# Four graph-attention layers by gathered neighbour lists: feature tables in rank order for the later layers, and masks gathered into that order

## The chip, the cores and the metric

The kernel runs on one core of a Trainium2 chip. A core has a matrix engine (PE), a vector engine (DVE), a scalar engine (ACT), GpSimd (POOL) and a sync engine (SP), which all run their own instructions in order and wait for each other by semaphores. DMAs are issued from the queues of SP, ACT and POOL and are carried out by 16 DMA engines. The metric is the device time of one execution in microseconds; the figure quoted is the median of several runs.

## The reference

Four layers of graph attention on 3327 nodes with 512 features. The adjacency matrix is symmetric, holds ones on its diagonal and is sparse: a node has between some ten and some forty neighbours. Each layer normalises, projects, scores every pair that is joined, takes a softmax over the neighbours, sums their projected features with these weights and adds the result to its input. The layers have 8, 4, 1 and 8 heads; layers two and three apply an ELU.

```python
h = jnp.maximum(_layernorm(x, axis=-1), 0.0)
...
Wh = (H @ W).reshape(n, N_HEADS, D_K)
sl = jnp.einsum('nhd,hd->nh', Wh, a_l)
sr = jnp.einsum('nhd,hd->nh', Wh, a_r)
e = jax.nn.leaky_relu(sl[:, :, None] + sr.T[None, :, :], negative_slope=NEG_SLOPE)
e = jnp.where(mask[:, None, :], e, -jnp.inf)
alpha = jnp.nan_to_num(jax.nn.softmax(e, axis=2), nan=0.0)
out = jnp.einsum('nhm,mhd->nhd', alpha, Wh).reshape(n, OUT_DIM)
...
x = x + ...
```

## The kernel before

The nodes are padded to 3328, 26 tiles of 128. A first stage (`tile_gat_stack`, lines 560 to 777) reads the adjacency matrix once. POOL multiplies each row by descending node numbers (line 679), DVE takes the largest entries of it, and so every node gets the list of its neighbours' numbers. It also counts the neighbours, and from the counts every node gets a rank: rank 0 has the most. Lists are then put into rank order. `Slots` holds them as columns of indices: column k of tile t has the k-th neighbour of the 128 nodes of ranks 128 t to 128 t + 127, and CAPS[t] is the number of columns of that tile, 36 down to 11. Column 0 is the node itself. There are two copies: `idx` holds node numbers, `twice` holds them doubled, because the first layer's table `tabx` has two half-rows for each node: projected features with scores, and the input x. A list that is shorter than its tile's columns is filled up with row 3328, a padding row with a score that gives no weight.

A table row has 528 numbers, two halves of 256 features and 8 scores each: the scores of the node as a target stand from column 256, those as a neighbour from column 520. `tabx` is filled in node order by the first stage (`features`, line 664). The check for lists that are too long branches to another program, `tile_gat_dense`, which does not run with these inputs.

`tile_gat_lists` then runs the four layers. Its tiles are tiles of ranks, worked from 25 down to 0. A tile's columns are cut into groups of four (`Tile`, line 835). `fetch` gathers a group, one indirect DMA on POOL for each column (line 824); in the later layers the node's own row comes by a plain load from `own_d`, which is in rank order. `scored` computes the weights of a group (DVE, then one exp on ACT, line 880). `group` multiplies rows by weights (DVE, line 903) and adds them up with identity matmuls in one bank (PE, line 908). After the last group the steps of `ends` follow, spread over the next steps: mean, residual, normalisation, transposes, projection, and `rows` (line 976), which writes the next layer's row twice: plainly to `own_d` from SP, and by an indirect DMA from POOL (`scatter`, line 829) to the table of the next layer, `tabs`, which is in node order. Two such tables take turns. The last layer scatters its rows to the output in the same way.

A few tiles with the longest lists are not gathered in the later layers: 1, 9 and 2 of them in layers two, three and four. They go over the whole table, tile by tile, with masks (`Several`, `Wholes`), beside the gathering. The masks come from nine entries `Mask` among the first layer's steps: an entry gathers 128 rows of the adjacency matrix by rank, turns them on PE, and writes them as bytes to DRAM, with the rows in node order as the table has them. `Own` is used only if the first layer had such a tile; it has none.

The order is written out by hand for POOL, PE, DVE and ACT (line 1316); SP's order is left to the compiler. In the loop from line 1366 step s first fetches groups until LOOK = 7 steps ahead, then does what was put at its places "first", "scored" and "last". There are seven buffers `g` for groups. A tile's rows are written five steps after its mean, and its scatter stands in POOL's order there, behind the gathers of step s + 6. A layer's gathers read the whole table, so that the first of them waits for all 26 scatters of the layer before.

The lines that set the order of fetches and scatters:

```python
                while fetched < min(len(steps), s + LOOK):
                    steps[fetched][0].fetch()
                    fetched += 1
                do("first")
                if s + 1 < len(steps):
                    steps[s + 1][0].scored(steps[s + 1][1])
                do("scored")
```

Of the kernel before, what the change touches and what calls it, by code (L numbers as in the profile page):

```python
# [11 lines left out]
U8 = mybir.dt.uint8  # L12
# [483 lines left out]
class Slots:  # L496
# [3 lines left out]

    class Part:
# [13 lines left out]
    def __call__(self, t, k, twice=False):  # L515
        for p in self.parts:
            for t0, t1, n, c in p.blocks:
                if t0 <= t < t1:
                    at = c + (t - t0) * n + k
                    return (p.twice if twice else p.idx)[:, at:at + 1]  # L520
# [3 lines left out]
def tile_gat_stack(ctx: ExitStack, tc: tile.TileContext, x, adj, adjT, ws, avs, out):  # L524
# [35 lines left out]
    with ExitStack() as c1:  # L560
# [49 lines left out]
        def late_constants():  # L610
            pad = once.tile([1, 2 * ROW], F32, name="pad")
            nc.gpsimd.memset(pad, 0.0)
            nc.gpsimd.memset(pad[:, ROW - 8:ROW], FAR)
            nc.sync.dma_start(tabx[NP:NP + 1, :], pad)
# [49 lines left out]
        def features(t, vx, xn, ve):  # L664
# [3 lines left out]
                                 scale=rstd)  # L668
            nc.sync.dma_start(tabx[t * P:(t + 1) * P, :], vx)

        count, pieces, last, normed, loads = None, [], None, None, []
        with tc.manual_schedule(engines={mybir.EngineType.Pool, mybir.EngineType.DVE}):
            for t in range(NT):
# [33 lines left out]
                nc.gpsimd.memset(vx[:, ROW + F:], 0.0)  # L707
# [8 lines left out]
        with tc.manual_schedule(engines={mybir.EngineType.Pool, mybir.EngineType.PE,  # L716
# [7 lines left out]
            nc.vector.tensor_add(rank, rank, part)  # L724
            hi = small.tile([P, NT], F32, name="hi", bufs=1)
# [60 lines left out]
def tile_gat_lists(ctx: ExitStack, tc: tile.TileContext, x, adj, ws, avs, out, ident, half, slots, L, low, spare, tabx, tabs):  # L786
# [25 lines left out]
    own_d = [[dram.tile([P, ROW], F32, name=f"own{i}_{t}") for t in range(NT)] for i in range(2)]  # L812
    tabs_v = [dram_disjoint_views(t[:, :], NT) for t in tabs]
    wide = 3 * P
    masks = [dram.tile([NT, P, wide], U8, name=f"mask{p}") for p in range(ND // 3)]
# [19 lines left out]
    class Tile:  # L835
# [10 lines left out]
        def fetch(self):  # L846
# [6 lines left out]
            for q in range(n):  # L853
                if l > 0 and k0 + q == 0:
                    nc.sync.dma_start(g[:, 0, :], own_d[l % 2][t])
# [9 lines left out]
        def scored(self, i):  # L865
# [4 lines left out]
            if i == 0:  # L870
# [4 lines left out]
                nc.vector.tensor_copy(self.s, g[:, self.own, F // 2:F // 2 + H])  # L875
# [5 lines left out]
            if self.l == 0 and i == 0:  # L881
                nc.scalar.activation(xs[self.t], g[:, n, :F], AF.Copy)
# [93 lines left out]
        def rows(self):  # L976
            if self.W is not None:
                v = scaled(nc, self.pv, self.rstd, work)
                nc.sync.dma_start(own_d[(self.l + 1) % 2][self.t], v)
                waiting.append((tabs_v[(self.l + 1) % 2][self.t], self.t, v))  # L980
# [18 lines left out]
    class Mask:  # L999
# [23 lines left out]
        def keep(self, c0, c1):  # L1023
            def piece():
                u = L.bitcast(U8)[:, c0 * P:c1 * P]
                nc.scalar.activation(u, self.pt[:, :(c1 - c0) * P], AF.Copy)
                p, q = divmod(self.t, 3)
                nc.sync.dma_start(masks[p][c0:c1, :, q * P:(q + 1) * P].rearrange("j p c -> p j c"),
                                  u.rearrange("p (j c) -> p j c", c=P))
            return piece  # L1030

        def finish(self, s):
            for i, c0 in enumerate(range(0, NT, 7)):
                c1 = min(c0 + 7, NT)
                later(s + 1 + i, "first", self.turn(c0, c1))
                later(s + 1 + i, "last", self.keep(c0, c1))

# [7 lines left out]
    class Wholes:  # L1045


        def __init__(self, l, W):
            self.l, self.tiles = l, [Whole(l, t, W) for t in range(ND)]
            self.s = pools["e"].tile([P, ND], F32, name="s", bufs=1)  # L1050
            for t in range(ND):
                nc.sync.dma_start(self.s[:, t:t + 1], own_d[l % 2][t][:, F // 2:F // 2 + 1])
# [13 lines left out]
        def load(self, p, j):  # L1066
# [3 lines left out]
            nc.sync.dma_start(mk, masks[p][j])  # L1070
# [72 lines left out]
    class Own:  # L1143


# [288 lines left out]
```

## Time and profile before

| | |
|---|---|
| median of 3 runs | 2498.1 us (2496.62 to 2504.0) |
| the profiled execution | 2956.34 us |
| its span, first to last instruction | 2954.6 us |
| first stage | 0 to about 262 us |
| the four layers | 262 to 1090, 1096 to 1802, 1806 to 2293, 2297 to 2955 us |
| granted PE clock, mean | 0.88 |
| moved by DMA | 612.95 MB |

The profiled execution is 18% longer than the runs that are timed, so that shares and sequences can be read from it, and durations only with care. A row of the page has the line, the engine, the operation, what is written and read, then busy time, mean duration in ns, and the idle time of that engine just before, with what ended it. "issue" is time in which nothing visible was waited for. The page's split of POOL's work by line, apart from those rows that the prediction shows:

```profile
L824 POOL DMA_INDIRECT g<-tabx,twiceb x342 | 325.1, 951 | 142.2 <-issue 94.6
L824 POOL DMA_INDIRECT g<-tab,idxa x297 | 285.0, 960 | 151.6 <-issue 83.8
...
L679 POOL TENSOR_TENSOR key<-a,keys 128x3328 int32<-128x3328 int32 (+1 forms) x29 | 189.3, 6530 | 2.6 <-DVE cand L688 1.3
```

By layer the gathers of table rows are 467, 406, 243 and 382 (columns of the gathered tiles, less the plainly loaded own rows), in 133, 118, 72 and 111 groups.

### The profile page before, as it was taken

The page shows a single profiled execution, that of the slowest core. Times are in us where ns is not written, and L with a number is a line of the kernel's source. Part 1 is how long each engine was busy: PE and PEld are TensorE (multiplying, and loading weights), DVE is VectorE, ACT ScalarE, POOL GpSimd, SP SyncE. Part 2 cuts the span into 40 slices and gives each one's busy share as a digit, 9 for nine tenths or more (in the row PEclk, how much of TensorE's full clock was granted, in tenths as well). Part 3 has the DMA queues.
Part 4 walks back from the last instruction along what each step waited for, and adds up shares of the span by engine and source line. Part 5 has one row for each costly group of instructions (what it writes and reads, how often), then busy time and mean ns, then how long its engine had stood idle before and what let it go on. Part 6 is the DMA issues. An engine that isn't in the chain of part 4 may idle for free. (4 is left out here: it accounts for less than half of the span.)

```text
span 2954.6 us, 26562 instructions
## 1 busy us (share of the span) xinstructions
PE 2226.0 (75%) x6832; PEld 1218.4 (41%) x6832; DVE 1929.8 (65%) x5004; ACT 895.5 (30%) x2347; POOL 1772.6 (60%) x1777
## 2 busy tenths in 40 slices
PE   4776777777766766888878885768795578887887
PEld 2653344433433333444434442334354344444443
DVE  7997756555545545677756664887888366665666
ACT  5881122221221112333322222333333233332321
POOL 7994566666556636666655644565654565655664
PEclk9998889888888888899988988879898788997899
DMA  6985677777666646777766755777775676666774
GB/s 244 330 300 160 185 235 224 235 221 229 197 203 189 197 125 206 221 209 210 205 199 197 216 163 169 228 227 249 213 253 154 190 208 193 203 195 183 206 199 129
DMA packets 253737, 612.95 MB, mean 207 GB/s; under 512 B 91011, under 2 KB 108419, under 8 KB 249222
## 3 DMA queue, kind: packets, MB, share of 16 engines
q0 software_dynamic: 131120, 455.33, 51.9%
q1 hardware_dynamic: 118710, 149.01, 15.8%
q10 hardware_dynamic: 3744, 6.82, 0.7%
q8 instruction: 55, 0.90, 0.1%
q14 instruction: 108, 0.88, 0.1%
HBM read 544.13 MB, written 66.89 MB: 207 GB/s over the span
## 5 line engine op out<-in xcount | busy, mean ns | idle before, releaser
L908 PE MATMUL bank<-m,ident 128*128 128x512 f32 x2608 | 1313.0, 651 | 319.2 <-DVE m L903 173.2
L903 DVE TENSOR_TENSOR m<-g,pw 128x512 f32<-128x512 f32 x1304 | 811.2, 682 | 523.6 <-ACT pw L880 268.8
L824 POOL DMA_INDIRECT g<-tab,idxb x734 | 703.2, 958 | 386.8 <-issue 201.4
L908 PEld LDWEIGHTS bank<-m,ident 128*128 128x128 f32 x2608 | 522.6, 208 | 970.0 <-issue 642.2
L469 PE MATMUL pv<-w,hT 128*128 128x264 f32 x1664 | 434.3, 417 | 77.8 <-ACT hT L458 37.7
L469 PEld LDWEIGHTS pv<-w,hT 128*128 128x128 f32 x1664 | 337.8, 206 | 182.4 <-issue 48.3
L824 POOL DMA_INDIRECT g<-tabx,twiceb x342 | 325.1, 951 | 142.2 <-issue 94.6
L824 POOL DMA_INDIRECT g<-tab,idxa x297 | 285.0, 960 | 151.6 <-issue 83.8
L880 ACT ACTIVATE pw<-z 128x32 f32<-128x32 f32 (+5 forms) x434 | 83.5, 192 | 885.1 <-DVE z L879 376.0
L1107 PE MATMUL whole<-ve,em 128*128 128x512 f32 x468 | 232.6, 647 | 51.5 <-issue 21.6
L832 POOL DMA_INDIRECT tab<-v,idxb x54 | 54.1, 1003 | 234.2 <-ACT v L476 193.7
L679 POOL TENSOR_TENSOR key<-a,keys 128x3328 int32<-128x3328 int32 (+1 forms) x29 | 189.3, 6530 | 2.6 <-DVE cand L688 1.3
L898 DVE SCALAR_TENSOR_TENSOR bank<-g,pw,bank 128x512 f32<-128x512 f32 x243 | 183.3, 754 | 11.2 <-DVE bank L898 2.6
L451 PE MATMUL pt<-ident,xn 128*128 128x128 f32 x416 | 72.1, 301 | 134.4 <-ACT xn L487 46.5
L1107 PEld LDWEIGHTS whole<-ve,em 128*128 128x128 f32 x468 | 93.9, 207 | 167.2 <-issue 124.8
L688 DVE MAX8 cand<-key 128x8 f32<-128x208 int32 x416 | 143.9, 364 | 0.1
L877 DVE TENSOR_TENSOR z<-g,pw 128x32 f32<-128x32 f32 (+5 forms) x434 | 74.6, 172 | 105.4 <-DMA g<-tab,idxa 61.2
L824 POOL DMA_INDIRECT g<-tabx,twicea x99 | 94.8, 957 | 79.7 <-issue 39.4
L451 PEld LDWEIGHTS pt<-ident,xn 128*128 128x128 f32 x416 | 53.0, 153 | 176.9 <-issue 54.3
L476 ACT ACTIVATE v<-pv,rstd 128x528 f32<-128x528 f32 x78 | 54.2, 695 | 215.4 <-PE bank L908 75.6
L458 ACT ACTIVATE hT<-pt 128x512 f32<-128x512 f32 x104 | 61.1, 587 | 175.0 <-remote 107.5
L1248 ACT ACTIVATE spare<-room,low 128x64 f32<-128x64 f32 x208 | 58.0, 337 | 175.3 <-PE bank L908 86.0
(172 smaller groups left out, 2204.1 us busy)
## 6 DMA issues: line engine op xcount, KB each, us to landing
a<-in_adj SPq DMA_DIRECT2D x25, 1664.0 KB
own<-v SPq DMA_DIRECT2D x78, 264.0 KB
ve<-tab SPq DMA_DIRECT2D x78, 264.0 KB
g<-own SPq DMA_DIRECT2D x66, 264.0 KB
tabx<-vx SPq DMA_DIRECT2D x26, 528.0 KB
g<-tab,idxb POOLq DMA_INDIRECT x734
low<-tab SPq DMA_DIRECT2D x52, 132.0 KB
room<-tab SPq DMA_DIRECT2D x52, 132.0 KB
```

The lines of the kernel that those rows point to most:

```text
L451: nc.tensor.transpose(pt[:, k, :], xn[:, k * P:(k + 1) * P], ident)
L458: nc.scalar.activation(hT, pt, AF.Relu)
L469: nc.tensor.matmul(pv[:, s, :HF + 8], hT[:, k, :], W.w[:, k, s, :], start=(k == 0), stop=(k == KC - 1))
L679: nc.gpsimd.tensor_tensor(key[:, c:c + quarter], a[:, c:c + quarter], keys[:, c:c + quarter], OP.mult)
L688: nc.vector.max(cand[:, g * 8:(g + 1) * 8], key[:, g * SEG:(g + 1) * SEG])
L824: nc.gpsimd.indirect_dma_start(out=out_, out_offset=None, in_=table, in_offset=bass.IndirectOffsetOnAxis(ap=which, axis=0))
L877: nc.vector.tensor_tensor(z, g[:, :n, ROW - 8:ROW - 8 + H], self.s.unsqueeze(1).to_broadcast([P, n, H]), OP.add)
L880: nc.scalar.activation(self.wt[:, k0:k0 + n, :H], z, AF.Exp)
L898: nc.vector.scalar_tensor_tensor(acc, v, w, acc, OP.mult, OP.add)
L903: nc.vector.tensor_tensor(m[:, q, :].rearrange("p (s h d) -> p s h d", s=2, d=D), v.rearrange("p s (h d) -> p s h d", d=D), wt[:, k0 + q, ...
L908: nc.tensor.matmul(self.po, ident, m[:, q, :], start=(k0 + q == 0), stop=(k0 + q == K - 1))
L1107: nc.tensor.matmul(tl.po.rearrange("p (s m) -> p s m", s=2), e[:, q * P:(q + 1) * P], v.rearrange("p (s m) -> p s m", s=2)[:, :, :F // 2], ...
```

## The change

The tables of layers two to four are in rank order. A tile's new rows are then 128 neighbouring rows, and one plain DMA from SP writes them to the table; `own_d`, the scatter of rows and the views for it go. The tile's own row and the target scores are loaded from the same place.

The later layers' lists must then hold ranks and not nodes. The first stage writes each node's rank as a number into column 256 of its row in `tabx`, in place of its first target score (one DMA of 26 x 128 single numbers). The 16 columns behind x, which were set to zero by POOL, take a copy of the scores, made by ACT. In the first layer every gathered row so brings the rank of the neighbour along, and after a group's exp ACT copies these numbers, converted to integers, over the group's columns of `idx`. The first layer gathers by `twice` and by column 0, which stay.

The masks' rows must be in rank order too. `Mask` writes its bytes to `found`, with rows in node order. 26 new entries, `Ranked`, gather 128 rows of it (1152 bytes each) by column 0 on POOL into one of three slices of `spare`, and SP writes them to `masks`. Eight of them stand between the last eight groups of the first layer, 18 behind the last group. `Mask` entries stand 10 steps apart and not 11. `Own` goes.

```diff
@@ Slots
-    def __call__(self, t, k, twice=False):
+    def __call__(self, t, k, twice=False, count=1):
...
-                    return (p.twice if twice else p.idx)[:, at:at + 1]
+                    return (p.twice if twice else p.idx)[:, at:at + count]
@@ first stage
+            nc.gpsimd.memset(pad[:, F // 2:F // 2 + 1], float(NP))
...
+            nc.scalar.activation(vx[:, ROW + F:].rearrange("p (s n) -> p s n", s=2), pv[:, :, ROW // 2 - 8:ROW // 2],
+                                 AF.Copy, scale=rstd)
...
-                nc.gpsimd.memset(vx[:, ROW + F:], 0.0)
...
+            nc.sync.dma_start(tabx[:NP, :].rearrange("(t p) c -> p t c", p=P)[:, :, F // 2:F // 2 + 1],
+                              rank.unsqueeze(2))
@@ tile_gat_lists
-    own_d = [[dram.tile([P, ROW], F32, name=f"own{i}_{t}") for t in range(NT)] for i in range(2)]
-    tabs_v = [dram_disjoint_views(t[:, :], NT) for t in tabs]
-    masks = [dram.tile([NT, P, wide], U8, name=f"mask{p}") for p in range(ND // 3)]
+    found = dram.tile([NP, ND * P // 4], I32, name="found")
+    masks = dram.tile([ND // 3, NT, P, wide // 4], I32, name="masks")
@@ Tile.fetch
-                    nc.sync.dma_start(g[:, 0, :], own_d[l % 2][t])
+                    nc.sync.dma_start(g[:, 0, :], tabs[l % 2][t * P:(t + 1) * P, :])
@@ Tile.scored
-                nc.vector.tensor_copy(self.s, g[:, self.own, F // 2:F // 2 + H])
+                nc.vector.tensor_copy(self.s, g[:, n, F:F + H] if self.l == 0 else g[:, 0, F // 2:F // 2 + H])
...
-            if self.l == 0 and i == 0:
-                nc.scalar.activation(xs[self.t], g[:, n, :F], AF.Copy)
+            if self.l == 0:
+                ranks = n - (i == 0)
+                nc.scalar.activation(slots(t, max(k0, 1), count=ranks), g[:, :ranks, F // 2], AF.Copy)
+                if i == 0:
+                    nc.scalar.activation(xs[self.t], g[:, n, :F], AF.Copy)
@@ Tile.rows
-                nc.sync.dma_start(own_d[(self.l + 1) % 2][self.t], v)
-                waiting.append((tabs_v[(self.l + 1) % 2][self.t], self.t, v))
+                nc.sync.dma_start(tabs[(self.l + 1) % 2][self.t * P:(self.t + 1) * P, :], v)
@@ Mask.keep
-                nc.sync.dma_start(masks[p][c0:c1, :, q * P:(q + 1) * P].rearrange("j p c -> p j c"),
-                                  u.rearrange("p (j c) -> p j c", c=P))
+                nc.sync.dma_start(found.rearrange("(j p) c -> p j c", p=P)[:, c0:c1, self.t * n:(self.t + 1) * n],
+                                  u.bitcast(I32).rearrange("p (j c) -> p j c", c=n))
@@ new
+    class Ranked:
...
+        def __init__(self, j):
+            self.j, self.k0 = j, [0]
+
+        def fetch(self):
+            n = ND * P // 4
+            rows = spare[:, self.j % 3 * n:(self.j % 3 + 1) * n].bitcast(I32)
+            gather(rows, found, slots(self.j, 0))
+            nc.sync.dma_start(masks[:, self.j, :, :].rearrange("s p c -> p s c"),
+                              rows.rearrange("p (s c) -> p s c", c=wide // 4))
@@ the loop over layers
-                    steps.insert(18 + 11 * t, (Mask(t), 0))
-            if l == 0 and DENSE[l]:
-                steps.insert(10, (Own(wholes.tiles[0], wholes.s[:, 0, :]), 0))
+                    steps.insert(18 + 10 * t, (Mask(t), 0))
+                steps[-8:] = [s for i, step in enumerate(steps[-8:]) for s in (step, (Ranked(i), 0))]
+                steps += [(Ranked(j), 0) for j in range(8, NT)]
```

The loads of `Wholes` and `Several` take tables and masks from the new places, in the same sizes.

## Prediction

> **What bounds the kernel now.** I read the page first for the engines' totals, then the busy time in the four layer stretches, then the waits, then the timeline at the places that the change touches.
>
> ```profile
> PE 2226.0 (75%) x6832; PEld 1218.4 (41%) x6832; DVE 1929.8 (65%) x5004; ACT 895.5 (30%) x2347; POOL 1772.6 (60%) x1777
> ...
> L824 POOL DMA_INDIRECT g<-tab,idxb x734 | 703.2, 958 | 386.8 <-issue 201.4
> ...
> L832 POOL DMA_INDIRECT tab<-v,idxb x54 | 54.1, 1003 | 234.2 <-ACT v L476 193.7
> ```
>
> No engine is full on the page. POOL's 60% hides something: its indirect DMAs last 0.95 us, but the timeline shows them 1.25 us apart whenever nothing else stops them (0.30 us of "issue" after each), so 77% on this page would already be a full POOL.
>
> ```profile
> 1049.95 0.94 POOL L824 DMA_INDIRECT g<-tabx,twiceb  x1 [0.31 <-issue]
> 1051.20 0.95 POOL L824 DMA_INDIRECT g<-tabx,twiceb  x1 [0.30 <-issue]
> 1067.42 0.99 POOL L832 DMA_INDIRECT tab<-v,idxb  x1 [15.28 <-ACT pw L880]
> 1089.65 0.99 POOL L832 DMA_INDIRECT tab<-v,idxb  x1 [21.24 <-ACT v L476]
> 1096.61 0.99 POOL L824 DMA_INDIRECT g<-tab,idxa  x1 [5.98 <-DMA tab<-v,idxb]
> ```
>
> This is the seam between the first and the second layer: the last gather, two scatters that wait for their rows, then the next layer's first gather, 45 us later. The seam is the compute tail, not POOL's own work.
>
> ```profile
> 262.00:1090.00 828.00, 620.57 (x1740) 310.42 (x1738) 472.37 (x1260) 162.43 (x337) 478.30 (x502) 0.87 0.68 203
> 1096.00:1802.00 706.00, 561.99 (x1604) 298.52 (x1604) 446.78 (x1202) 202.16 (x613) 411.42 (x432) 0.89 0.67 196
> 1806.00:2293.00 487.00, 359.59 (x1027) 201.93 (x1026) 383.84 (x730) 170.32 (x414) 277.86 (x294) 0.86 0.72 224
> 2297.00:2955.00 658.00, 515.75 (x1660) 272.58 (x1660) 398.89 (x837) 182.06 (x633) 391.55 (x408) 0.87 0.66 191
> ```
>
> The columns are length, then PE, weight loads, DVE, ACT and POOL (busy us and count). At 1.25 us each POOL's instructions fill 628, 540, about 355 and 510 us of the four layers, PE's busy time 621, 562, 360 and 516: they are level in all four, and DVE (384) leads in the third.
>
> ```profile
> POOL tab L832 <- ACT v L476: 250.0, 50, 21.2
> POOL g L824 <- DVE m L903: 86.0, 51, 7.9
> ...
> DVE z L877 <- DMA g<-tab,idxa: 61.2, 7, 19.9
> ```
>
> POOL stands 250 us before scatters and 86 us and more before gathers whose buffer the compute still holds. DVE waits for gathered rows 61 us only, in seven places, nearly all at starts of layers. So in this execution gathers arrive in time, and a scatter that blocks POOL costs little: at its place in the order groups up to six steps ahead have been fetched (LOOK = 7, seven buffers), some 30 us of work.
>
> **The profiled time and the median.** The profiled execution took 2956.34 us (span 2954.6), the median is 2498.1: 458 us less. If all of that lies in the four stretches (2679 us), they last 2221 us unprofiled. POOL's 1.25 us x 1615 indirect DMAs are 2019 us, 91% of that, where they are 75% of the profiled stretches. PE's 2058 busy us are 93% at the profiled clock of 0.87. Assuming that neither pace shrinks, POOL is much nearer to being the limit in the run that counts than on the page, with PE beside it. This is an estimate and the weakest step here.
>
> **What the Trainium skill says.** "DMA: Bandwidth & Descriptors", section Issuing engine by pattern, gives indirect transfers to GpSimd and simple stores to Sync; the trace agrees, with 0.99 us of POOL for a scatter and 0.32 us of SP for the plain write of the same rows (own<-v). Its section Issuing engines are not separate DMA queues says that another issuing engine saves only the time to initiate a DMA; so bytes moved from POOL to SP don't by themselves relieve the 16 DMA engines, and the page counts both queues, 51.9% and 15.8%, against the same 16 engines. Its section Rules for kernel authors says a strided last dimension becomes one descriptor per element; the trace holds no such transfer of the rank column's length.
>
> **The change part by part.** Removed: 78 scatters, 26 each for the tables of layers two, three and four. The last layer's 26 scatters to the output stay. The plain own write becomes the table write, so SP's count there is unchanged and 78 x 264 KB (20.6 of 613 MB) are not written twice.
>
> (1) First layer: 26 scatters at 0.99 + 0.30 = 1.29 us free POOL of 34 us; eight of the new mask gathers stand between its last groups, 8 x 1.25 = 10 us. Net 24 us of POOL; with PE level beside it I take three quarters, -18 us (0 to -24).
>
> (2) Second layer: 34 us of POOL, 540 to 506, but PE at 562 doesn't move: I take 0.4, -14 us (0 to -34). Third: DVE is ahead, -5 us (0 to -15). Fourth: no scatter leaves it, 0.
>
> (3) The waits for v that go: worth 0 in themselves. What is late next is the free g buffer, at almost the same place.
>
> (4) Seams two and three: the scatter at 1801.95 is followed by its first dependent gather at 1805.66, 3.7 us; the plain write at 1801.70 let a load of the same rows start at 1803.73, 2.0 us. Two seams, -3 us.
>
> (5) Masks. The nine Mask steps now write node-ordered rows, the same 128-byte pieces. New: 26 gathers of 1152-byte rows by node, each followed by an SP write into rank order, through three slices of one buffer. No row shows this. A turn is a gather's landing (at most 3.95 us: the third gather of the second layer's first group starts at 1099.18, its reader on DVE at 1103.13), a plain write (2.0 us, from (4)) and some 0.3 us of hand-over: 6.2 us for three slices, 2.1 us each. Eighteen stand behind the last group: 38 us. Their cover is the seam, 45 us on the page, or about 30 if compute follows POOL closely (3.95 landing, some 5 for the group, 15 from the last product on DVE at 1074 to the row at 1089, 7 from scatter to gather). The last tile's table write stands on SP behind about twelve of these writes, and the next layer's first own row behind the last. Queued behind a waiting gather on POOL is all of the second layer. Bounds -5 (cover whole, landing 2 us earlier) and +60 (5 us each); I take +10.
>
> (6) List turning: 133 ACT copies of 128x4 or less, at the 0.19 us of the small ACT rows, 26 us on an engine with 162 busy of 828. Each stands behind the exp that DVE waits for, one step ahead of its use, so it is hidden; were ACT's slack gone it would be 26 us. I take +2. They write idx columns that no gather of the first layer reads (those read twice, and column 0), so no gather waits for them.
>
> (7) Stage 0: 26 memsets (115 ns mean, some 0.19 with the gap) leave POOL, which paces that stage at 7.8 us a tile: -4 us (0 to -5). 26 small ACT copies, 5 us, go beside it: ACT is 86 of 100 us busy there, still under POOL. The rank column is 3328 four-byte pieces issued on SP near 246.7; the first gather goes at 262.2, and POOL stands 13 us at 291 because compute begins only at 298. So 15 to 28 us of cover; cost 0, and +15 if it takes 40 us.
>
> Sum: -18 -14 -5 -3 +10 +2 -4 = -32 us, 2498 to **2466**. Against the profiled execution, where compute leads, the same terms give less: 0 for (1) and (2), some -10 in all.
>
> **Rivals.**
> A, the forecast: POOL relief counts in part. 2466. For: the 91%. Against: the 61 us.
> B: compute sets the pace unprofiled as it does on the page; only seams and stage 0 gain, 2498 - 7 + 2 = 2493. For: POOL's waits for compute, over 300 us. Against: those waits are from an execution 18% too slow.
> C, slower: the mask chain between the first and second layers. POOL and SP are both in order, and the third gather back waits for an SP write that waits for a gather and for whatever stands ahead of it on SP. At 5 us each, 18 x 5 - 30 = +60 instead of +10: 2498 - 42 + 60 = 2516. It decides from about 4 us each (72 - 30 = 42). For: the seam has no other work, so all over the cover is on the path. Against: the pieces known add to 2.1 us.
> D: POOL is the whole limit, each of 78 scatters worth 1.29 us and a few us of lost lead: -101 - 7 + 20 = 2410.
> That the lists come out unturned would show as wrong rows, not as time.
>
> **How the numbers follow.** A 0.43, B 0.20, C 0.28, D 0.09. 0.3% is 7.5 us, about what a measurement here tells from no change. Faster: A, D and a third of B, 0.59. Same: half of B and a little of C, 0.14. Slower: the rest, 0.27. The range 2415 to 2525 takes in C at 5 us and most of D. The likeliest's own range is 2440 to 2490.
>
> **What would show it.** Right: no tab<-v on POOL; first-layer POOL count still near 502; mask gathers about 2 us apart in the seam and its length no more than 55 us; DVE's waits for g no longer than before. (1) and (2) are wrong if the second layer isn't shorter. (5) is wrong if these gathers stand over 4 us apart or the seam passes 70 us. (6) is wrong if DVE's wait for the exp of L880 grows over 269 us. (7) is wrong if the first gather starts after 275. The whole is wrong if the gathers turn out not to be paced at 1.25 us unprofiled.

## The result, and the profile after

The changed kernel takes 2491.9 us (median of 4 runs, 2489.5 to 2493.7), the kernel before 2497.4 (4 runs): ratio 0.9973, 95% interval 0.9951 to 0.9995. The forecast was 2466. About 5 us (1 to 12 by the interval) came of the 32 expected.

The profiled execution of the change took 2493.7 us. The profile first shown, of 2956, was no measure for it; the first experiment is the kernel before once more (`e0_before_again`, below), profiled in an execution of 2500.5 us, as long as the medians. All comparisons here are with that one. Cut at POOL's first and last gather of each layer, read off POOL's timeline, the two spans (first column of before) differ so, in us:

| stretch | before | changed | difference | foreseen |
|---|---|---|---|---|
| first stage, to the first gather | 265.0 | 282.3 | +17.3 | -4 |
| layer one, first to last gather | 640.4 | 614.3 | -26.1 | -18 + 2 |
| seam to layer two | 33.1 | 47.9 | +14.8 | +10 |
| layer two, first to last gather | 536.5 | 523.8 | -12.7 | -14 |
| seam | 33.4 | 33.7 | +0.3 | half of -3 |
| layer three | 422.6 | 422.8 | +0.2 | -5 |
| seam | 42.3 | 41.6 | -0.7 | half of -3 |
| layer four, to the end | 525.5 | 525.5 | 0.0 | 0 |
| span | 2498.8 | 2491.9 | -6.9 | -32 |

So the change does what it was said to do, and more in layer one. It is the first row that takes most of it back.

The page of the changed kernel, its totals and its largest group of gathers:

```profile
PE 2083.4 (84%) x6832; PEld 1163.5 (47%) x6832; DVE 1935.6 (78%) x5004; ACT 911.6 (37%) x2506; POOL 1710.7 (69%) x1700
...
L830 POOL DMA_INDIRECT g<-tab,idxb x734 | 698.2, 951 | 284.7 <-issue 173.1
```

No row writes `tab` from POOL any more; ACT has 159 instructions more (133 list turnings and 26 score copies). A gather still lasts 0.95 us with 0.30 of "issue" behind it. Busy time by stretch (length, then PE, weight loads, DVE, ACT, POOL, each with its count), layers one to four from first to last gather, first of before:

```profile
265.00:905.40 640.40, 562.15 (x1693) 283.73 (x1691) 461.67 (x1226) 158.38 (x330) 475.30 (x500) 0.96 0.85 260
938.50:1475.00 536.50, 495.58 (x1534) 268.61 (x1535) 433.18 (x1160) 193.76 (x600) 406.48 (x427) 0.98 0.85 254
1508.40:1931.00 422.60, 322.72 (x925) 177.39 (x926) 359.65 (x675) 156.45 (x385) 269.22 (x284) 0.88 0.80 249
1973.30:2480.20 506.90, 454.00 (x1638) 244.31 (x1638) 393.18 (x817) 179.77 (x631) 384.30 (x403) 0.98 0.82 243
```

then of the changed kernel:

```profile
282.30:896.60 614.30, 555.21 (x1706) 281.59 (x1705) 465.96 (x1234) 175.77 (x461) 457.34 (x483) 0.98 0.86 264
944.50:1468.30 523.80, 492.96 (x1528) 268.32 (x1529) 432.14 (x1159) 193.44 (x598) 384.01 (x405) 0.97 0.82 248
1502.00:1924.80 422.80, 322.87 (x925) 177.67 (x926) 359.61 (x675) 156.10 (x385) 248.54 (x265) 0.89 0.75 236
1966.40:2470.40 504.00, 455.50 (x1644) 245.70 (x1643) 392.73 (x818) 179.65 (x631) 381.56 (x402) 0.98 0.82 245
```

Read POOL's count, not its busy time. In layer one of before 500 instructions at 1.25 us are 625 of 640 us, 98%, where its busy time says 74%. In the changed kernel 483 are 604 of 614, again 98%: POOL sets the pace of this layer in both. In layer two 427 are 534 of 536 us before, all of it; 405 are 506 of 524 after. There 22 fewer would be 27 us, and half of that came: POOL's gaps that the trace puts down to DVE's multiply, which still holds a buffer, grew from 7.3 us (24, none over 0.3) to 20.2 (36, up to 2.9), so that compute stands close behind. In layer three 284 were only 355 of 423, so 19 fewer change nothing. Layer four is full as well (403, 504 of 507 us), and no scatter left it. "Perfetto Trace Analysis" of the Trainium skill, section Identifying the Most-Contended Engine, takes a GpSimd occupancy percentage as a fair measure of closeness to the limit; for this stream of indirect DMAs the trace disagrees: 74% was full.

The waits that the prediction watched, first of before:

```profile
DVE m L903 <- ACT pw L880: 148.0, 318, 6.5
...
POOL tab L832 <- ACT v L476: 90.4, 13, 23.7
```

and of the changed kernel:

```profile
DVE m L912 <- ACT pw L886: 131.5, 315, 4.5
...
DVE z L883 <- DMA g<-tab,idxa: 83.0, 15, 37.1
...
POOL g L830 <- DMA tab<-v: 40.6, 2, 32.7
```

DVE waits no longer for the exp than before, so turning the lists shows no cost. The one wait of 37.1 us is the seam to layer two. POOL's timeline there shows the 18 mask gathers behind the last group (columns: start, duration, instruction, idle time before it and what ended it):

```profile
896.59 0.95 POOL L830 DMA_INDIRECT g<-tabx,twiceb  x1 [0.31 <-issue]
897.84 0.95 POOL L830 DMA_INDIRECT spare<-found,idxb  x1 [0.30 <-issue]
899.73 0.94 POOL L830 DMA_INDIRECT spare<-found,idxb  x1 [0.94 <-DMA masks<-spare]
904.40 0.94 POOL L830 DMA_INDIRECT spare<-found,idxb  x1 [3.72 <-DMA masks<-spare]
...
935.67 0.94 POOL L830 DMA_INDIRECT spare<-found,idxa  x1 [0.50 <-issue]
944.54 0.94 POOL L830 DMA_INDIRECT g<-tab,idxa  x1 [7.92 <-DMA tab<-v]
```

and SP's queue at the same time:

```profile
916.97 20.57 SPq L1056 DMA_DIRECT2D masks<-spare  x11
937.71 0.36 SPq L1226 DMA_DIRECT2D spare<-masks  x1
938.46 0.36 SPq L1056 DMA_DIRECT2D masks<-spare  x1
...
939.40 0.52 SPq L988 DMA_DIRECT2D tab<-v  x1
```

The 18 gathers take 38 us, 2.1 each, as worked out. ACT had the last row ready at 918.4; its write was issued at 939.4, behind the mask writes, and the first gather of layer two waited for it.

### The profile page after: what moved, and what is told of

It is laid out like the page before. It is cut to its first block, busy times and chain, and to the rows that moved or that the text cites. A ratio compares the mean times of both kernels' runs of the same rounds, so it can differ in the third digit from the quotient of the medians.

```text
span 2491.9 us, 26810 instructions
## 1 busy us (share of the span) xinstructions
PE 2083.4 (84%) x6832; PEld 1163.5 (47%) x6832; DVE 1935.6 (78%) x5004; ACT 911.6 (37%) x2506; POOL 1710.7 (69%) x1700
## 5 line engine op out<-in xcount | busy, mean ns | idle before, releaser
L917 PE MATMUL bank<-m,ident 128*128 128x512 f32 x2608 | 1204.6, 608 | 132.6 <-DVE m L912 132.0
L917 PEld LDWEIGHTS bank<-m,ident 128*128 128x128 f32 x2608 | 483.3, 193 | 714.0 <-issue 347.5
L830 POOL DMA_INDIRECT g<-tab,idxa x297 | 283.6, 955 | 145.1 <-issue 78.2
L1133 PE MATMUL whole<-ve,em 128*128 128x512 f32 x468 | 222.4, 623 | 41.4 <-DVE em L1119 38.5
L1108 ACT ACTIVATE r<-low,mc,b 128x384 f32<-128x384 f32 x78 | 52.6, 674 | 153.5 <-DVE em L1119 116.6
L432 POOL TENSOR_TENSOR rstd<-ve,half 128x1 f32<-128x1 f32 x52 | 31.8, 611 | 107.3 <-DVE ve L970 61.7
L1242 ACT ACTIVATE r<-low,spare 128x256 f32<-128x256 f32 x208 | 98.9, 476 | 5.1
L885 DVE SCALAR_TENSOR_TENSOR z<-z 128x32 f32<-128x32 f32 (+5 forms) x434 | 78.8, 182 | 15.3 <-DVE z L883 0.4
```

Of the source, the lines that this page charges most:

```text
L830: nc.gpsimd.indirect_dma_start(out=out_, out_offset=None, in_=table, in_offset=bass.IndirectOffsetOnAxis(ap=which, axis=0))
L885: nc.vector.scalar_tensor_tensor(z, z, SLOPE, z, OP.mult, OP.max)
L917: nc.tensor.matmul(self.po, ident, m[:, q, :], start=(k0 + q == 0), stop=(k0 + q == K - 1))
L1133: nc.tensor.matmul(tl.po.rearrange("p (s m) -> p s m", s=2), e[:, q * P:(q + 1) * P], v.rearrange("p (s m) -> p s m", s=2)[:, :, :F // 2], ...
L1242: nc.scalar.activation(self.r[:, h, :], self.a[:, g, :], AF.Relu, bias=-1.0, scale=self.b[:, j, g:g + 1])
```

## The experiments

First gather is the end of the first stage; a layer is counted to the next one's first gather. All times in us; n is the number of runs in the median. The ratio is to the kernel before, run beside it (medians of 2496.4 to 2501.5). First gathers and layers are read from one profile each; runs with the same first stage differ in the first gather by up to 4 us (the changed kernel, e1, e2, e3 and e6; e4 and e7; e8 and e9).

| run | first gather | layer one | layer two | median (n) | ratio to before, 95% |
|---|---|---|---|---|---|
| changed kernel | 282.3 | 662.2 | 557.5 | 2491.9 (4) | 0.9973, 0.9951 to 0.9995 |
| e0_before_again | 265.0 | 673.5 | 569.9 | 2500.5 (1) | |
| e1_ranked_early | 283.6 | 667.2 | 557.5 | 2492.9 (5) | 0.9957, 0.9944 to 0.9971 |
| e2_ranked_beside | 282.9 | 667.7 | 557.0 | 2498.7 (21) | 0.9986, 0.9979 to 0.9994 |
| e3_no_ranked | 284.4 | 640.1 | 557.2 | 2468.2 (4) | 0.9859, 0.9843 to 0.9874 |
| e4_scores_by_dma | 278.7 | 665.9 | 557.0 | 2489.0 (10) | 0.9972, 0.9960 to 0.9984 |
| e5_memset_kept | 278.5 | 666.0 | 556.1 | 2490.6 (20) | 0.9972, 0.9963 to 0.9981 |
| e6_masks_in_two | 281.1 | 638.2 | 564.3 | 2475.0 (4) | 0.9906, 0.9884 to 0.9927 |
| e7_both | 274.6 | 638.2 | 564.4 | 2468.5 (4) | 0.9883, 0.9860 to 0.9906 |
| e8_sofar_on_dve | 279.3 | 665.8 | 556.5 | 2491.7 (22) | 0.9979, 0.9970 to 0.9987 |
| e9_masks_and_sofar | 281.8 | 636.6 | 565.3 | 2472.1 (5) | 0.9898, 0.9881 to 0.9916 |
| e10_all_three | 294.8 | 637.3 | 566.5 | 2487.0 (16) | 0.9965, 0.9953 to 0.9977 |
| e17_masks_copy_again | 264.5 | 637.2 | 563.8 | 2453.3 (5) | 0.9833, 0.9811 to 0.9856 |

Six runs fell on a chip that takes 2962 us for the kernel before, called the slow chip below. They are compared only with each other and with the profile first shown, an execution of the same length whose chip is not on record:

| run | first gather | layer one | layer two | median (n) | ratio to before, 95% |
|---|---|---|---|---|---|
| before (profile first shown) | 262.2 | 834.4 | 709.1 | | |
| e16_after_again (changed kernel) | 280.6 | 830.6 | 729.9 | 2990.4 (8) | 1.0110, 1.0070 to 1.0150 |
| e12_copy_alone | 278.0 | 822.4 | 708.6 | 2971.3 (20) | 1.0049, 1.0027 to 1.0072 |
| e14_copy_in_dram | 262.7 | 832.7 | 733.9 | 2978.4 (21) | 1.0057, 1.0036 to 1.0078 |
| e15_masks_copy_in_dram | 261.8 | 824.9 | 755.6 | 2996.9 (6) | 1.0103, 1.0054 to 1.0152 |
| e11_act_order | 286.7 | 831.2 | 731.6 | 3009.8 (6) | 1.0156, 1.0117 to 1.0196 |
| e13_masks_act_order | 288.5 | 797.9 | 758.6 | 3012.8 (6) | 1.0151, 1.0111 to 1.0191 |

### Where the difference lies: before once more

> The kernel before, unchanged, for a profile of an execution about as long as the median (2497 us). Theory M (seam): the change gains some 25 us inside the layers and gives most of it back at the first seam, where the last tile's table write stands behind the mask writes; then this profile shows its first gather near 280 us as in the changed kernel, a seam from the last gather of layer one to the first of layer two of about 45 us with under 20 us in which all engines stand, and layer one longer than the changed kernel's 636 us (282 to 918) by 10 to 20 us. Theory S (first stage): the change makes the first stage some 15 to 20 us longer (score copies on ACT, rank column) and gains that back later; then the first gather here is near 263 us. Theory B (compute sets the pace): first stage and all four layers agree within 5 us each with the changed kernel's.

The first stage ended at 265.0 and layer one took 673.5, 11 us more than the changed kernel's. So theory S holds, and theory M in part: both the first stage and the seam give back.

### The masks: off the seam, and left out

e1 puts all 26 entries between the last 26 groups:

```diff
-                steps[-8:] = [s for i, step in enumerate(steps[-8:]) for s in (step, (Ranked(i), 0))]
-                steps += [(Ranked(j), 0) for j in range(8, NT)]
+                steps[-NT:] = [s for i, step in enumerate(steps[-NT:]) for s in (step, (Ranked(i), 0))]
```

> The changed kernel with all 26 Ranked entries between the last 26 groups of layer one, none behind the last group. Theory M: the 27 us in which all engines stand at the first seam shrink to about 10, and the time falls by 15 to 20 us against the changed kernel, to 2472 to 2477, 0.990 to 0.992 of before. Theory S and theory B: the seam isn't what costs; the lookahead of the last groups is halved (an entry counts as a step), so 2490 or a few us more, 0.997 to 1.001. A cost of that halved lookahead under theory M: up to 10 us given back in the end of layer one, 2482.

e2 fetches them beside those groups, with no steps of their own:

```diff
-                steps[-8:] = [s for i, step in enumerate(steps[-8:]) for s in (step, (Ranked(i), 0))]
-                steps += [(Ranked(j), 0) for j in range(8, NT)]
+                beside = {len(steps) - NT + j: Ranked(j) for j in range(NT)}
...
                     steps[fetched][0].fetch()
+                    if l == 0 and fetched in beside:
+                        beside[fetched].fetch()
```

> The changed kernel with the 26 mask gathers and writes fetched beside the last 26 of layer one's fetches, with no steps of their own, so that the lookahead stays seven groups. Theory M: 2468 to 2475, 0.988 to 0.991, and the last tile's table write is issued within 1 us of its row. Theories S and B: 2490 to 2495, 0.997 to 0.999. If POOL is the limit in the end of layer one, the 18 moved gathers cost 18 x 1.25 = 22 us there and the gain is gone.

In e3 `Mask` writes straight into `masks`, and `Ranked` goes:

```diff
-                nc.sync.dma_start(found.rearrange("(j p) c -> p j c", p=P)[:, c0:c1, self.t * n:(self.t + 1) * n],
+                p, q = divmod(self.t, 3)
+                nc.sync.dma_start(masks[p, c0:c1, :, q * n:(q + 1) * n].rearrange("j p c -> p j c"),
                                   u.bitcast(I32).rearrange("p (j c) -> p j c", c=n))
...
-                steps[-8:] = [s for i, step in enumerate(steps[-8:]) for s in (step, (Ranked(i), 0))]
-                steps += [(Ranked(j), 0) for j in range(8, NT)]
```

> The changed kernel without the 26 mask gathers and writes: Mask writes its bytes straight into the masks, with rows in node order, as the kernel before did. What is left out is the gathering of the masks into rank order, so that the tiles worked by masks in layers two to four get masks in another order than the table's. Theory M: the whole of the mask chain is gone, 10 POOL instructions fewer in layer one and no chain at the seam: 2462 to 2472, 0.986 to 0.990. Theories S and B: 2488 to 2492, 0.996 to 0.998.

Leaving the chain out saves 22 us of layer one, as theory M wanted. But moving it off the seam saves nothing: layer one took 5 us more in e1 and in e2. Theory M, that SP's queue at the seam was the loss, fell. POOL's timeline of e2 around the last group:

```profile
918.76 0.95 POOL L830 DMA_INDIRECT spare<-found,idxa  x1 [0.30 <-issue]
920.01 0.95 POOL L830 DMA_INDIRECT g<-tabx,twiceb  x1 [0.30 <-issue]
921.26 0.94 POOL L830 DMA_INDIRECT spare<-found,idxa  x1 [0.30 <-issue]
950.58 0.94 POOL L830 DMA_INDIRECT g<-tab,idxa  x1 [28.37 <-DMA tab<-v]
```

The seam is short again, from 920.0 to 950.6, but the last group goes 23.4 us later than in the changed kernel: 18 gathers at 1.25 us are 22.5. The last clause of e2's expectation is what came. A mask gather costs its place on POOL at all three places that were tried in layer one, and the seam was the cheapest of them.

### The masks in layer two

e6 leaves eight entries behind the last group and fetches 18 beside every second group of layer two, where the one masked tile needs them bit by bit:

```diff
-                steps[-8:] = [s for i, step in enumerate(steps[-8:]) for s in (step, (Ranked(i), 0))]
-                steps += [(Ranked(j), 0) for j in range(8, NT)]
+                steps += [(Ranked(j), 0) for j in range(8)]
+            beside = {8 + 2 * i: Ranked(8 + i) for i in range(NT - 8)} if l == 1 else {}
...
                     steps[fetched][0].fetch()
+                    if fetched in beside:
+                        beside[fetched].fetch()
```

> The changed kernel with eight Ranked entries behind the last group of layer one and the other 18 fetched beside every second group of layer two (from its ninth on), where the masked tile of that layer reads them only later. Theory P (POOL's 1.25 us per indirect DMA is the whole limit in layer one, so a mask gather costs its full time wherever it stands there, but only about 0.36 of it in layer two, where taking 34 us of POOL away saved 12): layer one as without masks, 640 to 645 us to the next layer's first gather and not 662, layer two some 8 us longer, 2476 to 2482, 0.991 to 0.994. Theory Q (POOL is the limit in both layers): layer two 20 us or more longer, 2488 to 2494. Theory R (the seam's chain alone was the loss): layer one 645, layer two unchanged, 2468 to 2474.

Layer one 638.2, layer two 6.8 us longer, 2475.0: theory P, each 1 to 2 us better than it said. Without the moved gathers POOL's instructions are 506 of layer two's 524 us, so there was room for most of the 22.5 us.

### The first stage: four edits that didn't settle it

e4 takes the score copy off ACT and writes the scores from SP by a second DMA; e5 keeps the copy and puts the memset back:

```diff
@@ e4
-            nc.scalar.activation(vx[:, ROW + F:]...)
-            nc.sync.dma_start(tabx[t * P:(t + 1) * P, :], vx)
+            nc.sync.dma_start(tabx[t * P:(t + 1) * P, :ROW + F], vx[:, :ROW + F])
+            nc.sync.dma_start(tabx[t * P:(t + 1) * P, ROW + F:].rearrange("p (s n) -> p s n", s=2),
+                              vx[:, :ROW].rearrange("p (s n) -> p s n", s=2)[:, :, ROW // 2 - 8:])
@@ e5
+                nc.gpsimd.memset(vx[:, ROW + F:], 0.0)
```

> The changed kernel with the copy of the scores taken off ACT: SP writes the same 16 numbers of each row to the table from where they stand already, by a second DMA of 128 x 2 pieces of 32 bytes a tile. Theory S1 (the copy on ACT, and the order that the compiler gives ACT with it, hold up the first stage; POOL's next key stands behind a rstd that waits for ACT): tiles of the first stage return to 7.8 us from some 8.6, first gather at 265 and not 282, time 2473 to 2478, 0.990 to 0.992 of before. Theory S2 (what holds it up is that the memset on POOL went, which had spaced the loads; or the larger traffic): no change, first gather at 278 or later, 2488 to 2495. Theory S3 (small pieces are dear on the queues): as S2 or worse, over 2495.

> The changed kernel with the memset of the 16 columns put back on POOL where it stood; ACT's copy then writes the same columns. Theory S1: the first stage stays long, first gather at 280 to 287, 2492 to 2497, 0.997 to 0.999. Theory S2: the first stage is as before, first gather near 266, 2474 to 2478, 0.990 to 0.992.

Either edit brought the first gather only to 278.6, little more than such profiles differ by. Neither S1 nor S2 came out as put. e7 joined e4 and e6, and the gains added (28 us of e4's 7 and e6's 21):

> The changed kernel with both edits: scores written to the table by SP's own DMA, and 18 of the mask gathers moved to layer two. Theories S1 and P add: 2458 to 2466, 0.984 to 0.987 of before. If only one of them holds, 2473 to 2482. If neither, 2488 to 2495.

In the next cuts `key` is POOL's long product with the node numbers, `ve` the variance of a tile's rows, which ACT makes, `rstd` the factor that POOL makes of it, and `sofar` ACT's copy of the running counts, which come from PE (`count`). The timeline of ACT in one tile of the changed kernel's first stage:

```profile
205.63 0.21 ACT L646 ACTIVATE sofar<-count 128x41 f32<-128x41 f32 x1 [2.27 <-PE count L643]
205.73 0.69 ACT L669 ACTIVATE vx<-pv,rstd 128x528 f32<-128x528 f32 x1
...
206.44 0.27 ACT L671 ACTIVATE vx<-pv,rstd 128x16 f32<-128x16 f32 x1
...
207.68 0.22 ACT L492 ACTIVATE ve<-squares 128x1 f32<-128x1 f32 x1
```

and of POOL in the same tile:

```profile
199.35 7.25 POOL L683 TENSOR_TENSOR key<-a,keys 128x3328 int32<-128x3328 int32 x1
207.98 0.55 POOL L432 TENSOR_TENSOR rstd<-ve,half 128x1 f32<-128x1 f32 x1 [1.38 <-DVE cand L692]
208.49 7.25 POOL L683 TENSOR_TENSOR key<-a,keys 128x3328 int32<-128x3328 int32 x1
```

POOL waits 1.38 us for `ve` (which ended at 207.90; the profile names DVE, done long before), and ACT had stood 2.27 us at `sofar` ahead of it. In the kernel before, ACT:

```profile
210.65 0.21 ACT L644 ACTIVATE sofar<-count 128x41 f32<-128x41 f32 x1
...
213.02 0.20 ACT L492 ACTIVATE ve<-squares 128x1 f32<-128x1 f32 x1
```

and POOL:

```profile
207.01 7.32 POOL L679 TENSOR_TENSOR key<-a,keys 128x3328 int32<-128x3328 int32 x1
214.19 0.18 POOL L707 MEMSET vx<- 128x16 f32 x1
214.26 0.62 POOL L432 TENSOR_TENSOR rstd<-ve,half 128x1 f32<-128x1 f32 x1
```

`ve` is ready a microsecond before POOL is free, and POOL goes on without a gap, 7.78 us a tile. ACT's order isn't the same: before it is total, list, mean, running counts, xn, row, squares, `ve`, hT; in the changed kernel total, list, running counts, row, score copy, squares, hT, `ve`, then mean and xn. ACT and PE are ordered by the compiler in this stage. Between 100 and 240 us POOL waits 14.7 us in all before `rstd` in the changed kernel, 4.0 in the kernel before. Taking the running counts out of ACT's queue (e8) should have opened the circle that I saw here:

```diff
-                nc.scalar.activation(sofar, count, AF.Copy)
...
+                nc.vector.tensor_copy(sofar, count)
```

> The changed kernel with the copy of the running counts (sofar<-count, 128x41) made by DVE, beside the product that reads the same matmul's other half one tile later, and not by ACT. Theory L (loop through ACT's order): with the copies added the compiler gave ACT another order, in which sofar stands ahead of xn, ve of the same tile; so POOL's rstd waits for ve, ve for sofar, sofar for PE's count, count for DVE's o, o for POOL's key, and this circle takes 8.6 to 9.0 us where POOL alone takes 7.77. Taking PE's count out of ACT's queue opens the circle though ACT's score copies stay: tiles of 7.8 us, first gather at 264 to 268 and not 282, 2473 to 2478, 0.990 to 0.992 of before. Theory W (the work or the traffic added, or the lower PE clock of that stage, and not the order): no change, first gather 277 or later, 2488 to 2494. Theory D (DVE, 90% busy in that stage, becomes the bound with 26 more copies): tiles of 8.0 to 8.3, first gather 270 to 278, 2479 to 2487.

> The last edit together with the 18 mask gathers moved to layer two; scores still copied by ACT. Theory L: 2458 to 2462, 0.984 to 0.986 of before. Theory W: as with the moved mask gathers alone, 2472 to 2477, 0.990 to 0.991.

> The same with the scores written to the table by SP's own DMA and not copied by ACT. Theory L: no different from the copy on ACT by more than 2 us, since ACT is no longer late, 2457 to 2463. Theory W: 2465 to 2470, as with these two edits without the running counts on DVE.

279.3, 281.8 and 294.8: that wait went, others came, on x and still on `ve`, since the order changed again with the edit. Theory L as put, this one circle, fell. An attempt to write ACT's order by hand (e11, and e13 with the moved masks) moved PE's order along with it, so that PE stood 52 us before `pn` between 100 and 240 us; the first gather went at 286.7, and it told nothing of the order in question:

> The changed kernel with ACT's order of the first stage written by hand and not left to the compiler, every instruction kept, the score copies on ACT too: a tile's total, then the list and running counts of the tile two before, then mean, xn and ve of the tile itself, then the row and the score copy of the tile before, then hT; x is loaded one tile ahead. So ve stands 4 us or more before the rstd that reads it. Theory O (the loss is ACT's order, which the compiler changed when the copy came in): tiles of 7.7 to 7.9 us after the first eight, first gather at 262 to 270 and not 282, 2470 to 2480, 0.989 to 0.993 of before. Theory W (the work itself, the traffic or the lower PE clock): tiles stay above 8.3 us, first gather 277 or later, 2488 to 2495. If the hand order stalls at the start, where the weights arrive, the first eight tiles are longer and the gain is less; the later tiles' length still tells the two apart.

> The hand order of ACT in the first stage together with the 18 mask gathers in layer two. Theory O: 2453 to 2463, 0.983 to 0.987 of before. Theory W: 2472 to 2477.

### The first stage: the copy alone, and the order of before

e12 is the kernel before with the copy alone. e14 is the changed kernel with the scores copied inside the table by one DMA at the stage's end, and the memset back; in its trace the instructions of ACT, PE, DVE and POOL in the first stage stand in the same order as before, none more and none fewer.

```diff
@@ e12, on the kernel before
+            nc.scalar.activation(vx[:, ROW + F:].rearrange("p (s n) -> p s n", s=2), pv[:, :, ROW // 2 - 8:ROW // 2],
+                                 AF.Copy, scale=rstd)
@@ e14, on the changed kernel
-            nc.scalar.activation(vx[:, ROW + F:]...)
...
+                nc.gpsimd.memset(vx[:, ROW + F:], 0.0)
...
+            nc.sync.dma_start(tabx[:NP, ROW + F:ROW + F + 8], tabx[:NP, F // 2:F // 2 + 8])
             nc.sync.dma_start(tabx[:NP, :].rearrange("(t p) c -> p t c", p=P)[:, :, F // 2:F // 2 + 1],
```

> The kernel before with one part of the change alone: ACT's copy of the 16 scores behind x, after the memset of the same columns, which stays. Nothing reads the copies. Theory O: these 26 copies of 0.26 us give ACT the changed kernel's order and cost 12 to 20 us: first gather 277 to 285, 2508 to 2516, 1.005 to 1.008 of before. Theory W as far as it means the rank column, the missing memset or the other changes: first gather 263 to 268, 2495 to 2500, 0.999 to 1.002.

> The changed kernel with its first stage's engines as in the kernel before, ACT and PE in the same order, instruction for instruction: no score copy on ACT, the memset back on POOL. The scores are copied once, at the stage's end, by one DMA inside the table (3328 pieces of 32 bytes), ahead of the rank column, which waits for it. Theory O: tiles of 7.8 us, rank ready at 248 to 250; the two DMAs in a row take 2 x 6 us and end near 262, where lists are ready at 264: first gather 264 to 270, time 0.990 to 0.993 of before (2472 to 2480 where before is 2497). Theory W (traffic, the rank column, anything but the order): first gather 277 or later, 0.997 to 0.999. If the DMAs in a row take 20 us or more they show as a first gather behind 272.

> The changed kernel, unchanged, on the same chip as the two others, as their measure: 0.996 to 0.999 of before, first gather 280 to 284. On a chip whose executions are 18% longer, as that of the profile first shown, 1.000 to 1.010, since there POOL's cadence isn't the limit and the gathers wait for other engines.

On the same chip the copy alone moves the first gather from 262.2 to 278.0, and the whole change to 280.6 (262.2 is the profile first shown). Without it, with the rank column and all the rest in place, it goes at 262.7, and the time falls by 12 us against the changed kernel; it stays above that of the kernel before on this chip, where layer two is longer than before (733.9, 709.1). Busy time from 100 to 240 us of e12, with two waits of that stretch:

```profile
100.00:240.00 140.00, 102.55 (x448) 82.42 (x448) 116.22 (x571) 109.02 (x227) 127.24 (x50) 0.85 0.84 277
...
ACT sofar L644 <- PE count L641: 13.6, 10, 2.0
POOL rstd L432 <- ACT ve L492: 12.7, 14, 1.8
```

and of e14:

```profile
100.00:240.00 140.00, 103.72 (x508) 83.97 (x507) 126.76 (x626) 113.46 (x231) 130.49 (x52) 0.94 0.80 282
...
POOL rstd L432 <- ACT ve L492: 2.7, 2, 1.8
ACT sofar L646 <- PE count L643: 1.5, 3, 0.8
```

ACT is busier in e14, where the stage is faster (231 instructions in 140 us, not 227), and not full in either: it isn't the copies' 26 x 0.26 us = 7 us of work. Nor is it the score copying as such, since e4 has none on ACT, still gets another order, and keeps most of the loss; there too POOL waits before `rstd` for `ve` (ten times, 9.9 us), and ACT before that at `sofar`. Nor is it the landing of the rows' writes, which took 9.5 us in the changed kernel and 5.7 before (medians), but 3.8 in e4. The granted PE clock is lower where the stage is longer (0.85 in e12, 0.94 in e14), but it alone doesn't do it: e12's three tiles between 125 and 150 us take 8.3 to 8.5 us at a clock of 0.93, those of the kernel before between 160 and 180 us 7.8 at 0.90.

What e14 has and e4, e5, e8, e11 and e12 haven't is the order of before. So the copy is shown to bring the loss, and the waits show its way through ACT's queue to POOL. That the order alone would do it, without any added instruction, is argued and not shown: no run holds the copy in the order of before.

### Both causes mended

> The same together with the 18 mask gathers in layer two. Theories O and P add: 0.983 to 0.987 of before (2455 to 2464 where before is 2497). Theory W: 0.990 to 0.992.

> The kernel with the scores copied inside the table and 18 mask gathers in layer two once more, unchanged, since the chip of its first run took 18% longer for every kernel and there the mask gathers' place paid nothing. On a chip that runs before in about 2497 us theories O and P give first gather 264 to 268, the next layer's first gather 638 to 642 us later, 2455 to 2464, 0.983 to 0.987. On a chip that runs it in about 2960 us: 1.005 to 1.015, as the first time.

e15 and e17 are one kernel. On the slow chip the first stage was mended, and moving the masks made the kernel 18 us slower than e14: layer one is 8 us shorter, layer two 22 longer. On a chip that takes 2497.3 us for before, it takes 2453.3, 1.7% less: first gather at 264.5, layer one 637.2, layer two 563.8. Its layers one and two:

```profile
264.50:869.80 605.30, 548.46 (x1693) 279.22 (x1691) 461.68 (x1227) 175.14 (x461) 450.74 (x476) 0.98 0.87 265
901.70:1431.70 530.00, 491.56 (x1531) 267.96 (x1532) 433.40 (x1160) 193.93 (x600) 401.12 (x424) 0.98 0.85 255
```

476 of POOL's instructions in 605 us, 424 in 530: both layers are full at 1.25 us each (98% and 100%).

## Why the prediction was wrong

Step (7), the first stage, is the one that failed: "26 small ACT copies, 5 us, go beside it: ACT is 86 of 100 us busy there, still under POOL". The copies' work was sized nearly rightly (0.26 us each, 7 us), but a share of busy time says nothing of where an engine's queue stands. With the copy in, the compiler ordered ACT and PE otherwise, `ve` came behind waits on PE, POOL's `rstd` behind `ve`, and the next key behind `rstd`: 8.7 us a tile (median) where POOL alone needs 7.78, 17.3 us in all. The saving was mis-sized too: without waits a tile takes 7.72 to 7.75 us in the changed kernel, so a memset was worth some 0.05 us and all 26 a little over 1, not 4. The step was 21 us off, of 25 for the whole, and its own sign of being wrong, a first gather after 275, came. Its other half held: the rank column, 3328 pieces of four bytes, was issued at 266.2 with the lists ready at 280.9 and landed in 5.9 us, so it is hidden. One descriptor for each element, as the Trainium skill says of such a column ("DMA: Bandwidth & Descriptors", section Rules for kernel authors), fits the 3344 packets of under 512 bytes that the trace shows for its 3328 elements, and cost no time here.

Step (1) was right in kind and small in size: -26.1 with the list turning, against -16 and a bound of -24. I took three quarters of POOL's relief because PE was level on the page; in an execution as long as the median it isn't, and POOL counts in full: 17 instructions fewer at 1.25 us are 21 of the 26 us, and the rest goes with shorter waits for buffers that DVE's multiply still holds (15.5 us before, 8.0 after). The 61 us that DVE waited for gathered rows, my argument against it, are 206 in that execution. Step (2) was right for layer two (-12.7 for -14), though its 0.4 was taken and not worked out, so luck has a part in it; nothing came in layer three. Step (3) held: POOL stood 90 us before scatters for want of a row, 65 at the seams, 26 in layer three and none inside layers one and two. Step (4), -3 at two seams, gave -0.4.

Step (5): 18 gathers at 2.1 us, 38 us, and the last write behind the mask writes, all as worked out; the seam grew by 14.8 and not 10. Rival C's 5 us a gather did not come. What I didn't see is that the chain off the seam is no cheaper. Step (6) held.

Rival B has the right number, 2493, for the wrong reason: compute doesn't set the pace in layers one and two. The weakest step, POOL near its limit unprofiled, was the sound one. It holds on the chips of the medians: on the slow chip, where POOL's instructions at 1.25 us take up 604 of 781 us of layer one, the change makes the kernel slower by 1.1%. Why layer two is longer there by 21 us in the one profile stays open. So does which dependence in the new order costs how much in the first stage: one of them was opened in e8, which changed the order again, and the others not singly.

## What to carry to other kernels

Where the compiler orders an engine, an added instruction can cost more than its duration (here 26 copies of 0.26 us, 7 us of work, moved the end of the stage by 16): compare that engine's order before and after, and look for an in-order queue through which the engine that paces the stage is fed. Hold POOL's indirect DMAs against their cadence, not their busy time, layer by layer: a layer at 98% pays for each of them in full, and one may be moved to where POOL has room. Before sizing anything, ask whether the profiled execution is as long as the median.

## What the runs showed that I had not expected

One chip took 18 to 22% longer for the three kernels that also ran on others (2962 us for before, against 2496 to 2501; 2997 and 2453 for the one kernel of e15 and e17), and the first stage there is no longer than elsewhere (261.8 in e15, 264.5 in e17): the loss is in the layers, where the trace shows waits put down to nothing on the core, such as "ACT v L476 <- remote", 43 us in four waits of up to 19.6 between 285 and 890 us of e14. The faster executions of the kernel before, the changed kernel and e17 show no such wait there. What they wait for is not shown. On that chip the order of the two kernels is reversed (1.011 where it was 0.997).

A copy from DRAM to DRAM of 3328 pieces of 32 bytes landed in 4.7 and 5.1 us (e14, e17), no longer than the write of one tile's rows (5.3 in e17, median).
